# Filling the constant rows of layer 1's key tiles by ScalarE activations instead of by copies of whole tiles

## The chip, the core and the metric

The kernel runs on one core of a Trainium2 chip. Time is device time in microseconds (us) of that core, from three runs of the same program; one further execution was recorded by the hardware profiler, and all rows below come from it. The engines are TensorE (PE, with its weight loads as PEld), VectorE (DVE), ScalarE (ACT), GpSimd (POOL) and SyncE (SP). SP issues every transfer of this kernel, in order, on one queue; the transfers then run on 16 DMA engines.

## The reference, cut to what matters

Two transformer layers with adaptive layer norm, in 32-bit floats, on 2 sequences of 512 tokens and 512 channels. Each layer is an attention part and a feed-forward part, each behind a layer norm whose scale and shift come from a small conditioning vector, and each added to the residual through a gate.

```python
x = L0_attn_hidden_states                                   # [2, 512, 512]
h = _layernorm(x) * (1 + ca) + sa
x = x + ga * _L0_attn_ref(h, ...)      # 32 heads of 128, gated, decaying linear attention in chunks of 128
h = _layernorm(x) * (1 + cb) + sb
x = x + gb * _L0_ffn_ref(h, ...)       # sign of the weights
h = _layernorm(x) * (1 + ca) + sa      # from here on with layer 1's sa, ca, ga, sb, cb, gb
x = x + ga * _L1_attn_ref(h, ...)
h = _layernorm(x) * (1 + cb) + sb
x = x + gb * _L1_ffn_ref(h, ...)       # 4 streams, 50 rounds of Sinkhorn
```

The change is in layer 1's attention: 32 query heads of 16 channels, 8 key heads, each key head shared by 4 query heads, with a rotation by position and a softmax over all 512 keys.

```python
q = _rope(xq, cos, sin); k = jnp.repeat(_rope(xk, cos, sin), REP, axis=2)
scores = jnp.einsum('bqhd,bkhd->bhqk', q, k) / jnp.sqrt(jnp.float32(D))
probs = jax.nn.softmax(scores.astype(jnp.float32), axis=-1)
out = jnp.einsum('bhqk,bkhd->bqhd', probs, v)
```

## The kernel before

**Precision.** PE takes its operands in a shorter float (fp32r). Where that is too coarse, a value is split into a high part (an ACT copy into fp32r) and a low part (the rest, by POOL or DVE), and three products are summed: high by high, low by high, high by low. `halves` (L206) splits weights so, `exact` (L449) activations, `passes` (L226) makes the products.

**Layer 0's attention** is walked in 64 units, one for a group of four heads, a sequence and a chunk of 128 tokens (loop at L1374). A unit makes scores (`sps`), decays (`dec`, from `gb`, which SP broadcasts out of DRAM), mixes (`yps`), a gate (`gps`, `gate`, L471), a state (`cps`, `state`, L517), turns the result (`ztp`, `turn`, L562) and projects it out (`ops`, `project_out`, L577). `keys_of`, `query_of` and `values_of` project the next group's keys, queries and values (`pps`) meanwhile. Weights come from memory into the pool `raw` (four buffers, `raw_tile`, L198): `wk0`, `wq0`, `wv0` for the projections, `wg0` for the gate, `wo0` for the output. A buffer is free again when ACT has made the high part and POOL the low part.

**From layer 0 to layer 1.** With unit n goes `tail(n)` (L691): layer 0's feed-forward part and layer 1's norm, chunk by chunk. When the norm of a sequence is done, `project_kv` and `project_q` (L682, L686) project keys, values and queries of layer 1; `rope_halves` (L664) rotates them (shuffle and sums on DVE, one product on POOL), splits them into `hi1` (two buffers) and `lo1`, and writes both to DRAM, `k_dram` and `q_dram`, in an order of 48 rows a head (high, low, high for keys, high, high, low for queries), so that one matmul makes all three products. From unit 53 on (`FIRST`) pieces of layer 1's attention are worked beside the units.

**Layer 1's attention** goes through 16 entries of `order`: a sequence, half the queries, two of the 8 key heads. Each entry has two key tiles of 128 rows by 512 keys, one for each key head s (`ks`). `keys1` (L792) fills rows 48s to 48s+47 from `k_dram`; `queries1` (L799) fetches the query tiles `qs`. `maxima` (L833) makes scores `s` with rows 0 to 95 (L842) and their maxima `m` on DVE (L846); the negated maxima, split into high and low, go through PE (`mt`), ACT (`mm`) and a transfer (L862) into rows 96 to 99 of `qs`. `weigh` (L864) makes the scores again with 100 rows (L876), and ACT their exponentials `pt` (L881); `outputs` (L886) multiplies with the values into `op`. `weigh` runs up to 10 pieces behind `maxima` (`LAG`).

For this the key tiles need constant rows: zero where the other key head lies, zero or one in rows 96 to 99. Two rows of ones add the maximum's high and low part of that head. They are written once per tile, by `layer1_keys` (L740): for each s one load of a constant tile of 128x512 from DRAM (`c_keys1`) into `raw`, one ACT copy into a buffer of `hi1` (the local name is `empty`), and one transfer of the whole tile from there to each key tile. There are three sets of tiles, j = 0, 1, 2. Sets 0 and 1 are asked for at L711, within the loop over the two sequences in `tail`, so the call stands in the program twice; the second time gives new tiles, and those are used. Set 2 is asked for by the first `keys1` (L788). A tile is used again for later entries, with only its 48 rows replaced.

```python
KS, KM = 96, 100                 # rows of a key tile: keys; keys and constants
def key_tile(i):
    return i % 2 if i < TWO else (i - TWO + 2) % 3     # TWO is 0
...
if n == FIRST - 1:               # in tail(n), inside "for b in range(B)"
    layer1_keys()
```

**The feed-forward part of layer 1** (`streams0`, `streams1a`, `streams1b`, L1212 on) is a chain of small DVE and POOL instructions (the Sinkhorn rounds). The first half runs beside the attention; the last runs alone at the end and closes with PE and DVE products (`mix`).

**Order.** No queue's order is written out by hand. A planner places all instructions of all engines by its own estimates and by priorities (`tc.high_priority`); `anchor`, `behind` and `gated` add order without data, so that the work beside a unit keeps its place. `layer1_keys` at L711 stands within `behind`: its instructions may not be placed before the anchor of their engine. The call from `keys1` has no such bound. The rotation table of layer 0, `rope` (128x2x512, L353, loaded at L1339), stays in place to the end.

Of the kernel before, what the change touches and what calls it, by code (L numbers as in the profile page):

```python
# [9 lines left out]
FP = mybir.dt.float32  # L10
FR = mybir.dt.float32r
# [20 lines left out]
AF = mybir.ActivationFunctionType  # L32
# [4 lines left out]
P = 128  # L37
B, L, HID = 2, 512, 512
# [14 lines left out]
def tile_adaln(ctx: ExitStack, tc: tile.TileContext, a: dict, out: bass.AP):  # L53
    nc = tc.nc
# [24 lines left out]
    def keep(shape):  # L79

        m = int(np.prod(shape[1:]))
        t = room0[0:shape[0], used0[0]:used0[0] + m]
        used0[0] += m
        if len(shape) == 2:
            return t
        names = "abc"[:len(shape) - 1]
        return t.rearrange(
            f"p ({' '.join(names)}) -> p {' '.join(names)}", **{n: k for n, k in zip(names, shape[1:])}
        )
# [61 lines left out]
    def temp(shape, dt, name, bufs=2):  # L151
        return wk.tile(shape, dt, name=name, bufs=bufs)

    def bank(shape, name, bufs=2):
        return psp.tile(shape, FP, name=name, bufs=bufs)
# [42 lines left out]
    def raw_tile(load):  # L198
        raw = raws.tile([P, KC * P], FP, name="raw")
        nc.sync.dma_start(out=raw, in_=load)  # L200
        return raw
# [149 lines left out]
    gn = keep([P, 1])  # L351
    nc.sync.dma_start(out=gn, in_=a["gnorm"])
    rope = ck.tile([P, 2, L], FP, name="rope0")  # L353

    ps = bank([64, HID], "mps")
    for kc in range(KC):
# [334 lines left out]
    def tail(n):  # L691
# [4 lines left out]
        for b in range(B):  # L696
            c = n - ends[b]
            with behind():
                if -3 <= c < 1:
                    load_ffn(c + 3)  # L700
                    if c == -2:
                        load_ffn_rows(b)
                elif c == 5:
                    load_l1(b)
                elif 6 <= c < 8:
                    load_l1q(2 * c - 12)
                    load_l1q(2 * c - 11)
                    if c == 7:
                        load_rope1()
                if n == FIRST - 1:  # L710
                    layer1_keys()  # L711
# [24 lines left out]
    ksd = {}  # L736
# [2 lines left out]

    def layer1_keys(js=(0, 1)):  # L740
        for s in range(2):
            empty = temp([P, L], FR, "hi1")
            nc.scalar.copy(empty, raw_tile(a["c_keys1"][s]))
            for j in js:
                ksd[j, s] = temp([P, L], FR, f"ks{j}{s}")
                nc.sync.dma_start(out=ksd[j, s].bitcast(FP), in_=empty.bitcast(FP))

    steps = [(g, b) for g in range(KV0 - AHEAD) for b in range(B)]
    steps += [(g, b) for b in range(B) for g in range(KV0 - AHEAD, KV0)]
# [36 lines left out]
    def key_rows(i):  # L786
        j = key_tile(i)
        if j == 2 and (2, 0) not in ksd:  # L788
            layer1_keys((2,))
        return [ksd[j, s] for s in range(2)]  # L790
# [583 lines left out]
    for n, u in enumerate(units):  # L1374
        g, b, c = u["at"]
        s = n // NC
# [127 lines left out]
```

## Time and profile before

| What | us |
|---|---|
| Runs | 1404.83, 1406.62, 1407.78 (median 1406.62) |
| The profiled execution, and its span | 1401.8, 1400.0 |
| PE busy | 1245.7 (89%) |
| DVE busy | 1159.8 (83%) |
| ACT busy | 831.5 (59%) |
| POOL busy | 775.8 (55%) |

The page gives for each engine its busy time in the span. Its 40 slices are read as tenths:

```profile
PE   5979999999999999999988999799999889994128
DVE  7998668687677687787899977688799979898887
ACT  5457576476376466666665656557567467664128
PEclk9989999999999999999999999999999999997568
DMA  8022241231142343324333317523203231200001
```

A slice is 35 us. The first is the start, which loads; layer 0 fills slices 1 to some 30 with PE full; from slice 25 on layer 1's attention runs beside it, and alone from about slice 31; the last four slices are the Sinkhorn chain. PE reaches 9 in nearly all slices but the end. A group of instructions by source line, for instance, reads as line, engine, operation, what it writes and reads with sizes, how often, busy time, mean ns of one, and the idle time of the engine just before with what ended it; here the ACT copy, and the engine that is second busiest:

```profile
L743 ACT CAST hi<-raw 128x512 fp32r<-128x512 f32 x6 | 3.7, 616 | 5.5 <-DMA raw<-in_wv 5.0 <-DMA raw<-in_c_keys 0.4
L846 DVE TENSOR_REDUCE m<-s 128x1 f32<-128x512 f32 x256 | 166.4, 673 | 18.6 <-PE s L842 18.3
```

### The profile page before, as it was taken

To read this page: it belongs to the slowest core of one execution; us is meant where nothing else is said; L and a number is where in the kernel's file an instruction comes from. 1 tells how busy PE (TensorE), PEld (TensorE's weight loads), DVE (VectorE), ACT (ScalarE), POOL (GpSimd) and SP (SyncE) were. 2 spreads that over 40 slices of the span, in tenths; PEclk is the share of its full clock that TensorE was granted. 3 is DMA by queue.
4 is the path that set the end of the run, shared out by engine and by line. 5 is a ranking of instruction groups with operands and counts; after the bars stand their busy time and mean duration, and the time that the engine had idled before them with its cause. 6 is when DMAs were issued, how large, how long until landed. Compare 5 with 4: busy or idle time off the path is not lost. (4 is left out here: it accounts for less than half of the span.)

```text
span 1400.0 us, 22901 instructions
## 1 busy us (share of the span) xinstructions
PE 1245.7 (89%) x7168; PEld 992.1 (71%) x7168; DVE 1159.8 (83%) x2969; ACT 831.5 (59%) x2354; POOL 775.8 (55%) x1169
## 2 busy tenths in 40 slices
PE   5979999999999999999988999799999889994128
PEld 3758888788788778888866777577676666663117
DVE  7998668687677687787899977688799979898887
ACT  5457576476376466666665656557567467664128
POOL 4454374364264367577777748545242655558861
PEclk9989999999999999999999999999999999997568
DMA  8022241231142343324333317523203231200001
GB/s 256 23 65 60 88 121 30 68 107 53 53 118 57 92 120 106 98 68 124 118 114 91 98 53 241 170 67 91 90 24 113 71 111 52 59 11 1 1 16 46
DMA packets 95377, 117.13 MB, mean 84 GB/s; under 512 B 10828, under 2 KB 50508, under 8 KB 95256
## 3 DMA queue, kind: packets, MB, share of 16 engines
q1 hardware_dynamic: 95256, 115.67, 27.7%
q8 instruction: 57, 0.93, 0.3%
q14 instruction: 64, 0.52, 0.1%
HBM read 102.11 MB, written 10.64 MB: 81 GB/s over the span
## 5 line engine op out<-in xcount | busy, mean ns | idle before, releaser
L846 DVE TENSOR_REDUCE m<-s 128x1 f32<-128x512 f32 x256 | 166.4, 673 | 18.6 <-PE s L842 18.3
L67 ACT ACTIVATE pt<-s 128x512 f32<-128x512 f32 x256 | 136.9, 602 | 33.3 <-PE s L876 31.7
L447 POOL TENSOR_TENSOR q<-xcos,rot 128x512 f32<-128x512 f32 x64 | 92.8, 1450 | 61.6 <-DVE xcos L445 57.1
L67 ACT ACTIVATE sg<-sg 128x512 f32<-128x512 f32 x128 | 80.6, 632 | 68.5 <-DVE sg L478 66.8
L876 PE MATMUL s<-qs,ks 100*128 100x256 f32 x512 | 103.3, 306 | 11.0 <-DMA qs<-mm 7.4
L842 PE MATMUL s<-ks,qs 96*128 96x512 f32 x256 | 103.6, 437 | 9.7 <-DVE m L846 7.5
L515 POOL TENSOR_TENSOR gb<-gb,q 128x512 f32<-128x512 f32 x48 | 63.2, 1319 | 77.7 <-ACT gb L67 68.7
L232 PE MATMUL pps<-hh,wq_h 128*128 128x512 f32 x256 | 103.2, 403 | 1.7 <-ACT vT L766 1.1
L876 PEld LDWEIGHTS s<-qs,ks 100*128 100x128 f32 x512 | 80.9, 195 | 33.5 <-ACT pt L67 8.9
L232 PE MATMUL gps<-wg_h,hh 128*128 128x512 f32 x256 | 101.8, 400 | 2.9 <-ACT wg_h L209 2.7
L232 PE MATMUL ops<-wo_h,zh 128*128 128x512 f32 x256 | 101.5, 397 | 1.7 <-ACT zh L570 1.0
L232 PE MATMUL ops<-wo_h,zl 128*128 128x512 f32 x256 | 100.8, 394 | 0.7 <-DVE zl L571 0.7
L232 PE MATMUL pps<-hl,wq_h 128*128 128x512 f32 x256 | 101.3, 396 | 0.0
L232 PE MATMUL pps<-hh,wq_l 128*128 128x512 f32 x256 | 101.2, 395 | 0.0
L232 PE MATMUL gps<-wg_l,hh 128*128 128x512 f32 x256 | 101.2, 395 | 0.0
L232 PE MATMUL gps<-wg_h,hl 128*128 128x512 f32 x256 | 100.6, 393 | 0.0
L232 PE MATMUL ops<-wo_l,zh 128*128 128x512 f32 x256 | 99.9, 390 | 0.0
L67 ACT ACTIVATE dec<-dec,room 128x128 f32<-128x128 f32 x256 | 83.0, 398 | 21.8 <-POOL dec L495 21.7
L548 PE MATMUL yps<-v,dec 128*128 128x128 f32 x512 | 94.2, 280 | 1.8 <-DVE xcos L445 1.0
L495 POOL TENSOR_SCALAR_AFFINE_SELECT dec<-gb 128x512 f32<-128x512 f32 x64 | 49.1, 768 | 80.7 <-DMA gb<-g_dram 51.8
L522 POOL TENSOR_TENSOR xw<-v,room 128x512 f32<-128x512 f32 x48 | 55.2, 1163 | 68.5 <-ACT v L462 64.3
L558 DVE SCALAR_TENSOR_TENSOR z<-yps,ss,sg 128x128 f32<-128x128 f32 x256 | 71.9, 340 | 24.0 <-ACT ss L67 23.8
(323 smaller groups left out, 3968.5 us busy)
## 6 DMA issues: line engine op xcount, KB each, us to landing
gb<-g_dram SPq DMA_DIRECT2D x64, 256.0 KB
raw<-in_wq SPq DMA_DIRECT2D x56, 256.0 KB
raw<-in_wg SPq DMA_DIRECT2D x48, 256.0 KB
raw<-in_wo SPq DMA_DIRECT2D x48, 256.0 KB
raw<-in_wmod SPq DMA_DIRECT2D x40, 256.0 KB
qs<-q_dram SPq DMA_DIRECT2D x64, 96.0 KB
q_dram<-hi SPq DMA_DIRECT2D x16, 256.0 KB
raw<-in_wk SPq DMA_DIRECT2D x14, 256.0 KB
```

The source lines that it names most:

```text
L67: ins = nc.scalar.activation(o, i, func, **kw)
L232: nc.tensor.matmul(ps, lhsT=l, rhs=r, start=i == 0, stop=i == n - 1)
L447: nc.gpsimd.tensor_tensor(dst, sp(xc_), sp(rot), ALU.add)
L495: anchor["pool"] = nc.gpsimd.affine_select(out=dec, in_=gb, pattern=[[0, REP0], [1, P]], compare_op=ALU.is_ge, fill=-1e30, base=0, channel ...
L515: nc.gpsimd.tensor_tensor(gb, gb, q[:, c], ALU.mult)
L522: nc.gpsimd.tensor_tensor(xw, u["v"][:, c, :].unsqueeze(1).to_broadcast(sh4), wdc[:, c, r0:r0 + REP0].unsqueeze(2).to_broadcast(sh4), ALU. ...
L548: nc.tensor.matmul(yps[:, h, :], lhsT=u["pr"][:, h, :], rhs=u["v"][:, c, :], start=True, stop=not c)
L558: nc.vector.scalar_tensor_tensor(z[:, h, :], yps[:, h, :], ss[:, h:h + 1], sg[:, h * P:(h + 1) * P], ALU.mult, ALU.mult)
L842: anchor["pe"] = nc.tensor.matmul(ps, lhsT=st["qs"][rp][0:KS, i, qt * P:(qt + 1) * P], rhs=st["ks"][s][0:KS], start=True, stop=True,).ins
L846: anchor["dve"] = nc.vector.tensor_reduce(st["m"][:, 2 * qt + s, i:i + 1], ps, AX.X, ALU.max, negate=True).ins
L876: nc.tensor.matmul(ps[:, j, :], lhsT=st["ks"][s][0:KM, kt * P:(kt + 1) * P], rhs=st["qs"][rp][0:KM, i, :], start=True, stop=True,)
```

## The change

Two columns of 128 values (`empty`, one for each s) are loaded at the start from the first column of each constant tile. `layer1_keys` then writes each key tile with one ACT instruction: an identity activation of the first half of `rope`, times 0.0, plus the column as bias, so that each row of the tile holds its constant. The constant tiles' loads, the ACT copies into `hi1` and the transfers from there to the key tiles are gone. Where the function is called is unchanged.

```diff
     rope = ck.tile([P, 2, L], FP, name="rope0")
+    empty = keep([P, 2])
+    for s in range(2):
+        nc.sync.dma_start(out=empty[:, s:s + 1], in_=a["c_keys1"][s, :, 0:1])
...
     def layer1_keys(js=(0, 1)):
         for s in range(2):
-            empty = temp([P, L], FR, "hi1")
-            nc.scalar.copy(empty, raw_tile(a["c_keys1"][s]))
             for j in js:
                 ksd[j, s] = temp([P, L], FR, f"ks{j}{s}")
-                nc.sync.dma_start(out=ksd[j, s].bitcast(FP), in_=empty.bitcast(FP))
+                nc.scalar.activation(ksd[j, s], rope[:, 0, :], AF.Identity, bias=empty[:, s:s + 1], scale=0.0)
```

## The prediction

> **What bounds the kernel now.** I read the page's busy shares first: TensorE (PE) is busy 89% of the span, VectorE (DVE) 83%, ScalarE (ACT) 59%. So what delays PE for good costs time, unless it is PE's idle time anyway. Then the busy time by stage, because the change touches one place, the hand-over from layer 0 to layer 1 (the edited tiles are written from 840 us on). Columns: stretch, its length, then busy time of PE, weight loads, DVE, ACT, POOL, then granted clock, DMA share, GB/s.
>
> ```profile
> 800.00:830.00 30.00, 28.32 (x145) 23.69 (x144) 26.44 (x55) 19.04 (x58) 13.54 (x11) 1.00 0.24 70
> 830.00:850.00 20.00, 20.00 (x95) 16.51 (x95) 12.33 (x21) 11.65 (x22) 14.63 (x15) 1.00 0.45 146
> 850.00:870.00 20.00, 17.94 (x85) 14.69 (x83) 15.81 (x25) 13.54 (x35) 15.00 (x13) 0.91 0.72 232
> 870.00:890.00 20.00, 14.35 (x64) 11.14 (x62) 10.01 (x19) 4.91 (x17) 9.77 (x8) 0.90 0.77 235
> 890.00:910.00 20.00, 18.09 (x74) 13.36 (x72) 18.48 (x34) 15.00 (x42) 12.77 (x11) 0.93 0.44 121
> ```
>
> From 850 to 910 every compute engine sags, the transfers stand at 0.72 and 0.77, and the clock falls to 0.90. This is a stage that waits for transfers inside a kernel that does not. The waits from 835 to 910 say for which (waiter <- releaser: total, times, longest):
>
> ```profile
> ACT wg_h L209 <- DMA raw<-in_wg: 13.7, 3, 6.0
> DVE z L558 <- ACT ss L67: 6.0, 1, 6.0
> ACT hi L743 <- DMA raw<-in_wv: 5.0, 1, 5.0
> PE gps L232 <- ACT wg_h L209: 2.7, 1, 2.7
> PE ztp L566 <- DVE z L558: 2.7, 1, 2.7
> PE cps L232 <- DVE xwl L454: 2.1, 1, 2.1
> ```
>
> ACT stands behind the gate weights (wg), PE behind ACT. `hi L743` is the copy that the change removes; while it stands, ACT's queue stands. The order of SP's queue shows why wg is late:
>
> ```profile
> 844.48 3.59 SPq L746 DMA_DIRECT2D ks<-hi  x4
> ...
> 853.15 1.12 SPq L746 DMA_DIRECT2D ks<-hi  x2
> 854.36 1.34 SPq L678 DMA_DIRECT2D k_dram<-hi  x2
> ...
> 876.24 0.43 SPq L200 DMA_DIRECT2D raw<-in_wg  x1
> ...
> 882.62 0.53 SPq L746 DMA_DIRECT2D ks<-hi  x1
> ...
> 884.77 1.81 SPq L200 DMA_DIRECT2D raw<-in_wg  x1
> ```
>
> One queue, in order: key-tile copies stand ahead of the projected keys (854) and between the gate weights (876 to 885). PE after the first of its three stalls:
>
> ```profile
> 861.83 0.50 PE L232 MATMUL cps<-xwl,kth 128*128 128x512 f32 x1 [2.06 <-DVE xwl L454]
> 863.57 0.63 PE L232 MATMUL pps<-hl,wq_h 128*128 128x512 f32 x1
> 865.92 0.40 PE L232 MATMUL pps<-hl,wq_h 128*128 128x512 f32 x1
> ```
>
> After 2.06 us of idling a matmul takes 0.63 us, and 0.40 again some 4 us on.
>
> **What is removed.** layer1_keys runs three times (twice for tiles 0 and 1, once for tile 2): 6 loads of c_keys and 10 copies ks<-hi, 256 KB each, 4.2 MB. In 830 to 910 the rates above move 20 us x (146+232+235+121) = 14.7 MB, so 29% of the stage's bytes go; at 235 GB/s they are 17.8 us of transfers. On SP they took 6.8 us (ks<-hi) and 2.6 us (c_keys) between 836 and 888. On ACT six CASTs at 0.616 us go (3.7 us). Their tiles also shared two buffers, `hi1`, with the layer-1 projections, and the four `raw` buffers with the weights; both are relieved.
>
> **What is added.** Ten ACTIVATEs of 128x512, bias from a column, source in SBUF. The trace has none of that form: bounds are the CAST from SBUF (0.616) and L661's ACTIVATE with a bias column from PSUM (0.685); each occupies the queue 0.52 or 0.58 us until the next. I take 0.58, for the bias column: 5.8 us, 2.7 more than six CASTs at 0.52. And two loads of 128 four-byte elements, 0.33 to 0.49 us each on SP by the gnorm and gate loads.
>
> **What moves.** The planner places the whole kernel anew; the built order shows where.
> - Two ACTIVATEs (tile 2) go to the start, on ACT between the second and third chunk's ht. There ACT was free at 20.66 us. The gate load, issued at 15.27, was read at 21.77 without a wait; the columns, issued behind rope and two of the xin, about 14.6, should by that land by 21.1. So the third chunk is late by 1.2 to 1.6 us. Against that, hh of the fourth chunk now precedes an xn on DVE: in the trace ht was ready at 24.95 and its hh ran only at 27.17, so up to 1.8 us earlier. DVE is 98 to 100% busy from 20 to 60 us with the same work. Bounds -1.8 to +1.6; I take 0.
> - Eight go to about 803 to 810 us, 4.6 us where ACT has no gap (19.04 of 30 overall, full from 795 to 810). Behind them on ACT: rstd, sg, the state copy, ht, zh. Walking the new order with the trace's durations, zh moves from 807.0 to about 811, and zl on DVE ends near 812.9. PE, which used to take z at 809.6, now does the gate's and state's matmuls first and comes to z at 812.3. Bound: 0 to +1; I take 0. Placed later, they would have hit PE.
> - On SP, with the copies gone, k_dram is issued right after v_dram, and the four wg loads come before q_dram. Projected keys: hi at about 841 (its DVE sum ended at 840.8) instead of 853.0. Wg: they now wait for `raw` buffers that POOL's splits free, about 851 to 859, instead of 876 to 885.
> - On PE the gate's matmuls move ahead of pps<-wq,wk, and the first layer-1 score stands after 3747 matmuls instead of 3803.
>
> **The sum.** PE's idle time from 850 to 910 is 2.06 + 5.65 + 1.91 = 9.6 us. At the rate of 800 to 850 (1.68 in 50) 60 us would have 2.0 anyway: 7.6 to win. The slow clock: six 512-wide matmuls from 863.00 to 865.69 took 2.69 us against 6 x 0.227 = 1.36 at the usual pitch; likewise 5 from 884.16 (2.16 against 1.14) and 7 from 889.43 (3.56 against 1.59). Together 4.3. Ceiling 11.9 us. What is late next: POOL, whose splits, rope products and lo's queue up (I count 37 us of its work from 835 on, so the last q's lo near 872, against 875.5 to 876.8 now, but with the gate splits already done), and its q_dram writes must land before the first score. I leave one stall of the first kind, 2.06 + 1.33 = 3.4. Gain 8.5 us. Ends: 0 (all of it hidden) and 11.9.
>
> After 910 PE is at 94% to 1270, and the tail (1270 to 1400, a VectorE chain that starts when attention ends) keeps its order within a few places, so the gain carries through. Against the profiled execution, 1401.8 us (span 1400.0 and 1.8 around it): 1393.3. That execution lies 4.8 us under the median of the three runs, 1406.6; so in their terms **1398**.
>
> **A rule weighed.** Row: slow matmuls follow gaps of 2.06, 2.72 and 2.73 us. The Trainium skill (TensorE: Matmul & The Clock Gate, Part 1) lets the clock fall only after an idle window of about 3.4 us; by that these gaps would cost no clock and the sum would be 7.6 - 2.1 = 5.5, thus 1401. The measured rows decide. A rule against the change: ScalarE: Activation LUTs, Rules for kernel authors, sends adds and multiplies to VectorE. But from 800 to 830 DVE is busy 26.4 of 30 and ACT 19.0; by the rule, eight fills at hh's 0.43 would put 3.4 us onto the fuller engine, and the sum would fall to about 5.
>
> **The rivals.**
> 1. *The gap closes and is handed back* (20%). From 910 to 1270 DVE is busy 316.6 of 360 us and PE 337.2; maxima, weights and outputs wait on each other there, PE idles 22.8 us. If the earlier start only finds those waits longer, half or all goes: 1402 to 1407. For it: the same two engines stay full. Against: the order meets the old one again soon after (after 4106 matmuls), with the same work behind.
> 2. *Slower* (15%). From matmul 4660 to 5590 (about 1090 to 1240 us) the planner has shuffled scores and outputs. PE waits there 7.4 us in 8 goes for qs<-mm, the maxima's trip by DMA, out of 20 such issues; each lands in 1.9 us on the chain. If a shuffle leaves less between issue and use, each further exposure costs 1.9: five take the gain, six more than 0.2%, eight give 1406.6 - 8.5 + 15.2 = 1413. For it: these distances were only just long enough. Against: shuffles also lengthen them.
> 3. *More* (7%): the whole ceiling and the start's 1.8 us: 1393.
> 4. *It does not do what it says*: excluded, the built order has none of the 16 transfers, ten ACTIVATEs, two columns.
>
> **How the numbers follow.** My forecast, gain 5 to 12, has 58%: own range 1394 to 1402. What a measurement can tell from no change is 0.2%, 2.8 us. Rival 1 splits into 9% faster and 11% same. Faster 58 + 7 + 9 = 74%, same 11%, slower 15%. Range: down to rival 3 with a late shuffle in its favour (1390), up to all handed back with the start's 1.6 on top and a little of rival 2 (1409).
>
> **What would show it.** Right: L746 gone; ten L747 rows near 0.69 us; PE idle from 850 to 910 down from 9.6 to about 4, clock above 0.95; wg loads issued some 20 us earlier and ACT's 13.7 us wait for them nearly gone; the first `s` matmul near 872 to 878 instead of 897. Wrong: ht of the third chunk beyond 24 us; PE waiting for zl or cps near 812; the sag still there behind POOL; more than twelve waits of PE for qs<-mm.

## The result, and the profile after

The changed kernel takes 1412.97 us (median of six runs, 1411.92 to 1417.09) beside 1405.13 us for the kernel before on the same chip: a ratio of 1.0081, 95% interval 1.0056 to 1.0106. I had forecast 1398.0, 1390 to 1409, and faster. It is slower, outside the range. The profiled execution took 1411.92 us, with a span of 1409.9 us (before: 1401.8 and 1400.0), so the pair of traces shows 9.9 us of loss.

The same stretches of time that the prediction showed of before, in the changed kernel (columns: stretch, length, busy time of PE, weight loads, DVE, ACT, POOL, granted clock, DMA share, GB/s):

```profile
800.00:830.00 30.00, 30.00 (x156) 25.39 (x155) 24.46 (x53) 23.62 (x68) 13.20 (x11) 1.00 0.25 72
830.00:850.00 20.00, 20.00 (x96) 16.60 (x95) 10.67 (x22) 11.09 (x21) 15.82 (x16) 1.00 0.31 93
850.00:870.00 20.00, 18.66 (x97) 15.21 (x97) 15.63 (x28) 12.75 (x40) 16.84 (x13) 1.00 0.56 165
870.00:890.00 20.00, 12.98 (x48) 9.34 (x46) 14.84 (x24) 5.10 (x11) 10.77 (x8) 0.81 0.74 221
890.00:910.00 20.00, 15.09 (x59) 12.05 (x59) 14.98 (x27) 10.80 (x30) 10.04 (x9) 0.76 0.21 58
```

The transfers are fewer, and the sag has not gone: it has moved 20 us later and is deeper. PE idles 1.34 + 7.02 + 4.91 = 13.3 us from 850 to 910 (9.6 before), at a clock of 0.81 and 0.76. From 890 on the transfers stand at 0.21, so it is not bytes that PE waits for there. The waits from 835 to 910:

```profile
POOL dec L498 <- DMA qs<-q_dram: 10.1, 1, 10.1
...
PE sps L232 <- ACT qh L456: 9.3, 1, 9.3
ACT dec L67 <- POOL dec L498: 8.9, 2, 8.5
...
ACT wg_h L209 <- DMA raw<-in_wg: 4.6, 1, 4.6
```

ACT's wait for the gate weights has shrunk from 13.7 to 4.6 us, as forecast. A new chain stands in its place: PE waits 9.3 us for qh, ACT stands behind dec's exponentials, and those wait for POOL's `dec`, which waits 10.1 us for a transfer. The row names the transfer that landed last by the profile, but `dec` reads gb, the broadcast of the gate's running sum. SP's queue shows where the gb loads stood:

```profile
852.27 0.42 SPq L200 DMA_DIRECT2D raw<-in_wg  x1
...
861.17 0.56 SPq L200 DMA_DIRECT2D raw<-in_wg  x1
...
878.36 1.93 SPq L681 DMA_DIRECT2D q_dram<-hi  x2
880.39 1.33 SPq L200 DMA_DIRECT2D raw<-in_wo  x1
881.81 1.09 SPq L681 DMA_DIRECT2D q_dram<-lo  x1
882.96 1.34 SPq L496 DMA_DIRECT2D gb<-g_dram  x2
```

The wg loads moved some 20 us forward, from 876 to 885 down to 852 to 863. The first gb load for the same group of heads did not: 882.96 now, 883.92 in the kernel before, whose row is

```profile
883.92 0.80 SPq L493 DMA_DIRECT2D gb<-g_dram  x1
```

The gb loads now stand on SP's queue behind the rows of layer-1 queries on their way to q_dram. POOL got on with `dec` at 890.84, and PE, which had done its other work by then, took the scores' matmul at 894.91:

```profile
875.05 0.70 PE L843 MATMUL s<-ks,qs 96*128 96x512 f32 x2 [2.03 <-DMA qs<-q_dram]
...
894.91 0.80 PE L232 MATMUL sps<-qh,kh 128*128 128x512 f32 x1 [9.32 <-ACT qh L456]
```

To see where 9.9 us arise I follow rows that both traces have. Times in us; zh, the 51st, is ACT's L573 (before L570), rc is DVE's reciprocal of `finish`, L922 (L921), of which there are 32.

| | before | after | difference |
|---|---|---|---|
| PE's first ops | 111.4 | 114.3 | +2.9 |
| zh, the 45th | 684.7 | 689.1 | +4.4 |
| zh, the 51st | 790.7 | 790.8 | +0.1 |
| rc, the 5th | 1029.5 | 1032.8 | +3.3 |
| rc, the 7th | 1052.9 | 1056.2 | +3.3 |
| rc, the 15th | 1149.4 | 1155.7 | +6.3 |
| rc, the 32nd | 1273.7 | 1284.2 | +10.5 |

The start costs 3 to 4 us, and a stretch with idle time on PE before 790 takes it back. The hand-over (51st zh to 5th rc) takes 242.0 us instead of 238.8. The largest part, 7.2 us, is lost after 1053 us, 150 us behind the edit: 7th to last rc take 228.0 us instead of 220.8.

### The profile page after: what moved, and what is told of

Its sections match the earlier page's. It is cut to its first block, busy times and chain, and to the rows that moved or that the text cites. A ratio compares the mean times of both kernels' runs of the same rounds, so it can differ in the third digit from the quotient of the medians.

```text
span 1409.9 us, 22944 instructions
## 1 busy us (share of the span) xinstructions
PE 1256.2 (89%) x7168; PEld 997.5 (71%) x7168; DVE 1155.9 (82%) x2969; ACT 835.6 (59%) x2358; POOL 779.1 (55%) x1169
## 2 busy tenths in 40 slices
DMA packets 93362, 112.94 MB, mean 80 GB/s; under 512 B 10861, under 2 KB 50541, under 8 KB 93241
## 5 line engine op out<-in xcount | busy, mean ns | idle before, releaser
L551 PEld LDWEIGHTS yps<-v,dec 128*128 128x128 f32 x512 | 80.5, 196 | 13.9 <-issue 5.1
```

The lines of the kernel that those rows point to most:

```text
L551: nc.tensor.matmul(yps[:, h, :], lhsT=u["pr"][:, h, :], rhs=u["v"][:, c, :], start=True, stop=not c)
```

## The experiments

Three theories. *Theory 1*: at the hand-over one wait took the place of another, the gb loads behind the query writes. *Theory 2*: the planner's shuffle of the late stretch costs, and it would cost without the edit too. The third is the start. Below, "hand-over" is the 51st zh to the 5th rc and "late" the 7th to the last rc, each from the run's one profiled execution; times are medians.

| kernel | hand-over | late | time, us | ratio to before, 95% |
|---|---|---|---|---|
| before | 238.8 | 220.8 | 1401.9 to 1405.1 | |
| after | 242.0 | 228.0 | 1412.97 | 1.0081, 1.0056 to 1.0106 |
| e1 after, query writes of two groups off SP | 240.1 | 219.2 | 1402.65 | 1.0001, 0.9977 to 1.0025 |
| e2 before, columns only | 235.2 | 224.7 | 1407.02 | 1.0029, 1.0001 to 1.0057 |
| e3 before, called once | 240.3 | 220.9 | 1408.65 | 1.0035, 1.0007 to 1.0062 |
| e4 after, called once | 242.2 | 233.8 | 1417.41 | 1.0086, 1.0052 to 1.0119 |
| e5 before, late order shuffled | 243.8 | 228.9 | 1421.69 | 1.0125, 1.0094 to 1.0156 |
| e6 before, late order kept | 237.5 | 217.9 | 1405.71 | 1.0004, 0.9983 to 1.0025 |
| e7 after, late order of before | 243.3 | 221.0 | 1406.14 | 1.0015, 0.9989 to 1.0041 |
| e8 after, late order shuffled | 241.9 | 231.6 | 1414.52 | 1.0074, 1.0045 to 1.0103 |
| e9 before, copies doubled | 249.3 | 221.1 | 1412.43 | 1.0064, 1.0042 to 1.0086 |
| e10 after, all query writes off SP | 230.6 | 218.8 | 1397.50 | 0.9943, 0.9921 to 0.9966 |
| e11 before, once and writes off SP | 238.2 | 225.4 | 1403.64 | 0.9982, 0.9952 to 1.0013 |
| e12 after, five raw buffers | 239.9 | 223.6 | 1408.53 | 1.0043, 1.0015 to 1.0072 |
| e13 before, writes off SP | 245.2 | 222.4 | 1407.64 | 1.0034, 1.0014 to 1.0055 |
| e14 before, three groups off SP | 244.4 | 223.7 | 1405.68 | 1.0025, 1.0002 to 1.0048 |

One and the same program varies: 26 runs of before beside e1 to e4 lay between 1394.79 and 1411.26. A single profile therefore says where time went, and the medians say how much.

**e1, the gb loads set free.** In `rope_halves` of the changed kernel (`dst` is q_dram for `wq1`):

```diff
-                nc.sync.dma_start(out=dst[:, r:r + D1, :], in_=src.bitcast(FP))
+                (nc.sync if not (b == 0 and n == "wq1" and i >= 2) else nc.scalar if src is hi
+                 else nc.gpsimd).dma_start(out=dst[:, r:r + D1, :], in_=src.bitcast(FP))
```

> The changed kernel, but the layer-1 query rows of head groups 2 and 3 of the first batch row are written to q_dram from ScalarE's queue (hi) and GpSimd's queue (lo) instead of SyncE's, so that the two loads of the gate gb stand 15 places earlier on SyncE's queue. Theory 1 (at the hand-over one wait took the place of another: POOL's dec waits for gb, which stands on SP's queue behind these writes, and qh, sps and all of PE behind dec): PE's wait of 9.3 us at 885 to 895 shrinks to under 3 us, PE's idle time from 850 to 910 falls from 13.3 to under 8 us, and if that carries through, the time falls by 4 to 9 us, to 1404 to 1409. Theory 2 (the late stretch decides: the planner's shuffle of scores and outputs after 1040 us costs the 7 us, whatever happens at the hand-over): the gap closes all the same, but the time goes anywhere from 1403 to 1418, because the late order is shuffled anew. My prediction's theory (POOL itself is what is late): the wait for dec remains, 1413.

Measured: 1402.65, the whole loss gone. The gb loads go out at 869.73, and the 9.3 us wait of PE is no longer among the waits. But the trace does not put the gain where theory 1 had it:

```profile
870.00:890.00 20.00, 15.91 (x57) 12.04 (x58) 15.66 (x25) 8.89 (x26) 15.96 (x14) 0.83 0.80 249
890.00:910.00 20.00, 18.01 (x72) 12.80 (x71) 19.85 (x38) 10.88 (x36) 10.92 (x9) 0.83 0.31 92
```

PE's idle time from 850 to 910 falls to 6.4 us, and then it idles 6.4 us more from 910 to 980 (4.2 in the changed kernel); the hand-over takes 240.1 us. Counted from the 51st zh, e1 reaches the 56th 5.2 us sooner than the kernel before (97.6 us against 102.8) and the 5th rc 1.3 us later: what was won is handed back, as rival 1 has it. At the 7th rc e1 is 3.4 us later than before, and the changed kernel 3.3. Only behind that do they part: 219.2 us to the end against 228.0. Here a comparison of the built orders tells why: from matmul 4106 to the end PE's order in e1 is that of the kernel before, place by place, while in the changed kernel some 740 places from 4660 on hold another matmul, 680 of them up to 5590. (The expectation of e5 says 964; a count by place cannot give that, as 4660 to 5590 has 931 places.) A small edit at the hand-over had thrown the planner back onto the old late order. That is for theory 2, but e1 changes two things at once.

**e2, the start alone.** The kernel before with the two column loads, read by nobody:

```diff
+    emptyc = keep([P, 2])
+    for s in range(2):
+        nc.sync.dma_start(out=emptyc[:, s:s + 1], in_=a["c_keys1"][s, :, 0:1])
```

> The kernel before, with the two column loads of the change added at the start and nothing reading them: the start is planned anew, all 16 transfers of the key tiles stay. Theory 1: nothing at the hand-over changes in kind, 1403 to 1407. A third theory (the change's loss is the start: the trace of after is 3.6 us late at 185 us): 1408 to 1409, if it is the loads and not the two ACTIVATEs behind them; by theory 1 that lateness is gone before 780 us, as in the trace of after. Theory 2 (a shuffle anywhere costs or wins up to 8 us by chance): anywhere from 1397 to 1413.

Measured: 1407.02. The reshuffled start is 5 to 6 us late from 250 to 640 us, more than in the changed kernel, and 1.5 us at the 51st zh. So lateness at the start is taken back before the hand-over here too, and it is not what the change lost. What this trace loses, it loses late (224.7): 4.9 us behind 1234 us, where the clock stands at half for 13.7 us against 3.4 in the kernel before, with PE's order that of before. The last section shows the same of e11.

**e3 and e4, made once.** The call for tiles 0 and 1 stands in `for b`; here it is made for one b only, in the kernel before (e3) and in the changed one (e4):

```diff
-                if n == FIRST - 1:
+                if n == FIRST - 1 and b == 0:
```

> The kernel before, with the call that makes key tiles 0 and 1 made once instead of twice: 2 loads, 4 copies ks<-hi and 2 CASTs fewer (1.5 MB of the 4.2 MB), no ACTIVATE and nothing at the start. My prediction's theory (the transfers bound the hand-over): a third of its gain, 1402 to 1403. Theory 1 (the next wait stands right behind): 1404 to 1408. Theory 2: anywhere from 1397 to 1413, with the difference arising after 1040 us.

> The changed kernel with that call made once: four of the ten ACTIVATEs fewer, the two columns and the two fills at the start stay. Theory 1: POOL's dec still waits for gb, 1411 to 1415. If the ACTIVATEs at 803 to 810 us were the cost (2.3 us of ACT go): 1410 to 1411. Theory 2: anywhere from 1403 to 1418, and the time of the hand-over (to 1040 us) as in the changed kernel within 2 us.

Measured: e3 1408.65 and e4 1417.41. Neither removal helps. In e4, 0.7 us of ACTIVATE each for four instructions is gone and its hand-over takes 242.2 us beside 242.0 in the changed kernel, so nothing shows that the fills at 803 to 810 us cost; it loses 13 us late, in an order that differs from the changed kernel's in some 260 places. In e3 1.5 MB of transfers are gone, the hand-over takes 240.3 instead of 238.8, and its late order, which differs from before's in some 200 places, costs nothing in its trace (220.9): not every shuffle costs.

**e5 to e8, the late order by itself.** The edit of e1 with other conditions gives four kernels: before and after, each with the late order kept or shuffled. The conditions (written `hi`, `lo` for the rows that leave SP's queue, the others staying on it):

```diff
 e5 (before): b == 0 and n == "wq1" and i >= 3, hi rows to nc.scalar
 e6 (before): b == 0 and n == "wq1" and i >= 3, lo rows to nc.gpsimd
 e7 (after):  b == 0 and n == "wq1",            lo rows to nc.gpsimd
 e8 (after):  b == 0 and n == "wq1" and i >= 3, lo rows to nc.gpsimd
```

> The kernel before with all its transfers; only the hi rows of the layer-1 query group 3 of the first batch row go to q_dram from ScalarE's queue instead of SyncE's. On PE this moves 234 places at the hand-over (matmuls 3645 to 4106), and it happens to give a late order like the changed kernel's from matmul 4660 on (of the changed kernel's 964 places of difference to before, most are shared). Theory 2, now that e1, which has the late order of before, lost nothing after 1056 us: the late order alone costs 6 to 10 us, so 1409 to 1414, with the lateness arising between 1100 and 1245 us, although nothing of the change is in this kernel. Theory 1 (the change's fills and the hand-over cost): 1402 to 1406.

> The same edit on the lo rows, to GpSimd's queue: 323 places at the hand-over differ from before, and from matmul 4106 on PE's order is that of before. Both theories: 1400 to 1406. If e5 and this one are both slow, the edit at the hand-over costs and not the late order.

> The changed kernel, the lo rows of all four query groups of the first batch row written from GpSimd's queue: another hand-over than e1's, and from matmul 4106 on PE's order is that of before. Theory 2: as e1, 1400 to 1406, and nothing lost after 1056 us. Theory 1: it depends on the hand-over alone; POOL's wait for gb before dec is about as long as in the changed kernel, so 1410 to 1414.

> The changed kernel, the lo rows of group 3 alone written from GpSimd's queue: at the hand-over 6 places on PE differ from the changed kernel, and from matmul 4660 on it has the late order of e4 (the called-once one), not that of before. Theory 2: 1412 to 1419, 8 to 14 us of it lost between 1056 and 1275 us. Theory 1: within 2 us of the changed kernel's 1413, and whatever differs arises before 1040 us.

Measured: kept, 1405.71 (before) and 1406.14 (after); shuffled, 1421.69 (before) and 1414.52 (after). The late order costs, whether the change is in the kernel or not: the kernel before, with all its transfers and none of the edit, is 1.25% slower in e5, and the changed kernel is the same as before within what is measured once its late order is kept. Not all of e5's loss is late: its trace is 15.6 us longer than that of before, 8.1 of it late and 5.0 at the hand-over (243.8 us). The cleaner pair is e7 and e8, with hand-overs of 243.3 and 241.9 us: 8.4 us lie between their medians, 10.6 between their late stretches. Over all sixteen kernels the late stretch takes 217.9 to 225.4 us where PE's late order is before's (or e3's) and 228.0 to 233.8 us in the four shuffled ones. e7 was told apart from theory 1 as well: POOL still waits 10.5 us for gb there, and the time is not 1410.

What the shuffled order does is seen at 1110 to 1150 us, where the second batch row's layer-1 projection runs beside attention. PE's larger waits there, first in the kernel before, then in the changed kernel:

```profile
1121.51 0.69 PE L842 MATMUL s<-ks,qs 96*128 96x512 f32 x1 [3.30 <-DVE m L846]
...
1134.74 0.48 PE L876 MATMUL s<-qs,ks 100*128 100x256 f32 x2 [2.07 <-DMA qs<-mm]
```

```profile
1123.09 0.50 PE L877 MATMUL s<-qs,ks 100*128 100x256 f32 x2 [2.81 <-ACT os L909]
...
1139.01 0.77 PE L877 MATMUL s<-qs,ks 100*128 100x256 f32 x2 [2.62 <-DMA qs<-mm]
```

and e5:

```profile
1130.41 0.80 PE L842 MATMUL s<-ks,qs 96*128 96x512 f32 x1 [3.47 <-DVE m L846]
1145.20 0.48 PE L876 MATMUL s<-qs,ks 100*128 100x256 f32 x2 [4.12 <-DMA qs<-mm]
```

The first wait of e5, for m, the kernel before has too (3.30 us), so the shuffle did not bring it. The second wait is for the maxima's short transfer, mm, which goes out straight behind the last query writes of the second batch row. Changed kernel, SP's queue:

```profile
1131.27 1.21 SPq L681 DMA_DIRECT2D q_dram<-hi  x2
1132.58 0.59 SPq L681 DMA_DIRECT2D q_dram<-lo  x1
1134.05 0.67 SPq L863 DMA_DIRECT2D qs<-mm  x1
```

From its issue to PE's next matmul 4.96 us pass (6.12 in e5, from 1139.08), with the transfers at 0.63 from 1130 to 1139. In the kernel before it went out at 1130.99, ahead of two of those writes, and 3.75 us later PE went on, having waited 2.07 us. From 1050 on, PE waits for qs<-mm 7.1 to 7.5 us in eight goes in kernels whose order is kept (before, e1, e6), and 7.0, 12.0, 10.6 and 9.8 us in ten to twelve goes in the changed kernel, e4, e5 and e8. Stretches at half clock follow such gaps. With the clock records of the traces, PE's idle time and its busy time times one minus the clock come to 27.3 us late in before and 24.4 to 32.2 in the other kernels with the order kept (or e3's), and to 30.9, 37.2, 33.8 and 36.0 in the changed kernel, e4, e5 and e8. The two ranges meet. What is left of the late stretch, PE's busy time reckoned at full clock, keeps them apart: 192.1 to 193.9 us in the twelve kernels, 195.1 to 197.2 in the four. Why the same matmuls take longer in the shuffled order is not shown.

**e9, what bytes cost.** The kernel before with each copy made twice, the second from ScalarE's queue:

```diff
                 nc.sync.dma_start(out=ksd[j, s].bitcast(FP), in_=empty.bitcast(FP))
+                nc.scalar.dma_start(out=ksd[j, s].bitcast(FP), in_=empty.bitcast(FP))
```

> The kernel before with each of the ten key-tile copies made a second time, from ScalarE's queue: 2.6 MB more transfers in the stage that my prediction says waits for transfers, and from matmul 4246 on PE's order is that of before. My prediction's theory (the stage waits for transfers; 4.2 MB less is worth 8.5 us): 2.6 MB more cost about 5 us, 1407 to 1412, lost between 840 and 960 us. Theory 2 with the hand-over bound by its chain of waits, not by bytes: 1402 to 1406.

Measured: 1412.43, 0.64% slower, all of it at the hand-over (249.3 us, +10.5; late 221.1 as before). The waits from 835 to 910 and the stretch say by what:

```profile
ACT wg_h L209 <- DMA raw<-in_wg: 13.8, 2, 13.0
...
PE gps L232 <- ACT wg_h L209: 10.7, 1, 10.7
```

```profile
890.00:910.00 20.00, 14.06 (x51) 10.96 (x52) 10.14 (x18) 10.07 (x24) 12.40 (x11) 0.70 0.92 256
```

So the chain that I named in the prediction, transfers to wg to ACT to PE, grows when the kernel before is given more transfers: 2.6 MB on top cost 7.8 us by the medians, nearly what I had given for 4.2 MB less. That bytes alone do it is not shown. ScalarE issues ten more transfers here, and the gate weights that ACT waited for were issued at 888.74 (876.24 to 884.77 in the kernel before), behind query writes on SP's queue.

**e10, the loss undone.** The changed kernel with the condition `b == 0 and n == "wq1"`, hi rows to ScalarE's queue and lo rows to GpSimd's:

> The changed kernel, the hi rows of all four layer-1 query groups of the first batch row written from ScalarE's queue and the lo rows from GpSimd's: the loads of gb stand 23 places earlier on SyncE's queue than in the changed kernel, and from matmul 4106 on PE's order is that of before. Theory 1 in its weaker form (the late order cost the 7 us, the wait for gb the rest, and with it gone the transfers' removal pays): the stretch from 790 to 1030 us shrinks from 242 to 234 or less, 1396 to 1400. If the next wait in line (queries through q_dram, splits on GpSimd) takes its place again: 239 to 242 there, 1401 to 1406.

Measured: 1397.50, ratio 0.9943 (0.9921 to 0.9966): faster than both. The gb loads go out at 855.57 and 861.67 instead of 882.96, the late order is before's (218.8 us), and the hand-over takes 230.6 us, 8.2 less than before.

```profile
850.00:870.00 20.00, 19.66 (x102) 16.25 (x102) 18.05 (x26) 13.47 (x42) 19.98 (x16) 1.00 0.69 202
870.00:890.00 20.00, 14.00 (x48) 10.53 (x47) 19.25 (x30) 10.27 (x22) 12.00 (x12) 0.82 0.58 189
890.00:910.00 20.00, 17.91 (x82) 13.95 (x82) 17.71 (x40) 10.79 (x39) 12.99 (x10) 0.92 0.33 96
```

POOL's wait for gb is down to 2.6 us, and no wait of PE in 835 to 910 is longer than 2.3 us. The profiled execution is the fastest of ten (1391.80); by the medians the gain is 7.1 us. Of the 8.2 us at the hand-over, 4.0 are idle time of PE and 3.6 busy time lost to half clock. But the wait for gb is not what sets e10 apart from e1, where that wait of PE is gone too and the hand-over takes 240.1 us: POOL's `dec` ran at the same time in both (e1, then e10), though gb was issued 14 us sooner in e10.

```profile
884.29 1.23 POOL L498 TENSOR_SCALAR_AFFINE_SELECT dec<-gb 128x512 f32<-128x512 f32 x2
```

```profile
884.62 1.23 POOL L498 TENSOR_SCALAR_AFFINE_SELECT dec<-gb 128x512 f32<-128x512 f32 x2
```

What else it is in moving the writes of groups 0 and 1 that pays, no run here shows.

**e11 to e14, whose gain is that?** e11 is e3 with the edit of e1. e12 is the changed kernel with `RAW = 5`. e13 and e14 make e10's move in the kernel before: e13 for all query and key rows of the first batch row, e14 for query groups 0 to 2.

```diff
 e13 (before): b == 0,                          hi rows to nc.scalar, lo rows to nc.gpsimd
 e14 (before): b == 0 and n == "wq1" and i < 3, hi rows to nc.scalar, lo rows to nc.gpsimd
```

> The kernel before, tiles 0 and 1 made once, and the query rows of groups 2 and 3 written from ScalarE's and GpSimd's queues: 1.5 MB of transfers fewer and no fills on ScalarE, and from matmul 4240 on PE's order is that of before. Theory 2: nothing lost late, 1400 to 1406, in contrast to e3 (1408.7, made once, with another late order). If fewer transfers without fills pay: 1397 to 1400.

> The changed kernel with five buffers for raw weights instead of four, so that weight loads on SyncE's queue wait less for GpSimd's splits, and what stands behind them too; the order up to 800 us differs in 600 places on PE, and from matmul 4240 on it is that of before. Theory 2: nothing lost after 1056 us, 1400 to 1406. If waits for buffers are what holds the hand-over: 790 to 1030 us in 236 or less, 1396 to 1400.

> The kernel before with all its key-tile transfers; the rows of keys and queries of the first batch row are written to DRAM from ScalarE's (hi) and GpSimd's (lo) queues, as in e10 and the keys too; from matmul 4106 on PE's order is that of before. If e10's gain is that of the move of the writes alone: 790 to 1030 us in 229 to 233, 1395 to 1400 as e10. If it takes both, the move and the change's fewer transfers: 235 to 241 there, 1401 to 1406.

> The kernel before, the query rows of groups 0, 1 and 2 written from ScalarE's and GpSimd's queues, those of group 3 from SyncE's; from matmul 4567 on PE's order is that of before. The same two readings: by the move alone 230 to 235 in 790 to 1030 us and 1396 to 1401, by both together 236 to 241 and 1402 to 1406.

Measured: e11 1403.64, e12 1408.53, e13 1407.64, e14 1405.68; hand-overs of 238.2, 239.9, 245.2 and 244.4 us. The move of the writes without the change gains nothing (in e13 ACT waits 18.7 us for wg from 840 to 985, and POOL 14.4 us for gb). Fewer transfers without the fills, with two groups moved, gain nothing that is clear of noise (e11, ratio 0.9982, 0.9952 to 1.0013). e12's fifth buffer does not help either: its gb loads go out at 894.92, later than in the changed kernel, and more than 800 places before 800 us differ, so it is a weak test. So the gain stands only where both are, the change and all the query writes of the first batch row off SP's queue. e13 moves the key rows too and e14 leaves one group of queries where it was, so neither is e10's move to the letter, and that it takes both is likely, not shown.

## Why the prediction was wrong, step by step

- *What bounds the kernel* held in part. The stage waits for transfers: doubling the copies lengthened the hand-over by 10.5 us (e9), through the chain that I had read from the waits. How much of that is bytes and how much the place on SP's queue, e9 does not tell apart.
- *Removed and added* held. 117.13 MB became 112.94, L746 is gone. The ten fills take 718 ns each (705 to 754), above both rows that I bounded them with (616 and 685); taking four away did not shorten the hand-over (e4).
- *What moves.* Right: hi for k_dram at 841, the wg loads at 852 to 863 (forecast 851 to 859), the first layer-1 score at 875.05 (forecast 872 to 878; 897.1 before), PE 30.00 of 30 busy over the eight fills. The start lies outside its bounds, -1.8 to +1.6: it runs 3 to 4 us late from 171 to 676 us. The third chunk's ht, which I had late, is not why: it started at 20.64 us, and at 21.54 in the kernel before. The lateness cost nothing, because a stretch before 790 us had the slack, which I had not named.
- *The sum: "I leave one stall of the first kind, 2.06 + 1.33 = 3.4"*. This step failed first. I had found what the change moves forward, and looked for what is late next among POOL's splits and the query writes. I did not follow gb, an input of the group of heads whose gate weights now came 20 us sooner. It stood on the same queue behind those query writes, at 882.96, unmoved. The stall was 9.3 us and the hand-over gained nothing (242.0 against 238.8, where kernels with before's transfers lie between 235.2 and 245.2). That this wait alone held the gain back is not shown: with it gone and little else moved (e1) the hand-over still takes 240.1 us. In e10 it gains 8.2 us, close to the 8.5 of the sum, but not in the way of the sum: PE still idles 8.4 us from 850 to 910, where I expected about 4.
- *"After 910 ... so the gain carries through"*. This step failed by more. It rested on PE being full and the tail's order being kept; the late shuffle in between cost 7.2 us in the trace, and 8.1 in e5, which has none of the change. With the late order kept (e1, e7) the changed kernel is as fast as before within what is measured. So this step is the loss, and the step before it the missing gain.
- *Rival 2* named that shuffle, the place (1090 to 1240 us) and a time (1413; measured 1412.97), and I gave it 15%. Its mechanism was half of it: the waits for qs<-mm grew in e4, e5 and e8, by 2.4 to 4.6 us, but not in the changed kernel (7.0 us in ten goes; 7.4 in eight before), where the largest new wait was 2.8 us for ACT's os, and half clock grew most. That the time agrees is luck: its sum holds the gain of 8.5 us, which did not come, and eight more waits of 1.9 us for qs<-mm, which did not come either.
- *The rule weighed.* The rows again decide: half clock follows gaps of 2.03 to 2.81 us in the changed kernel, below the idle window of about 3.4 us that the Trainium skill asks for (TensorE: Matmul & The Clock Gate, Part 1). Its figure returns as the length of a stretch at half clock and as the step of the grid on which the clock changes, as the last section shows. The rule for VectorE was not tried.

Open: which of the shuffled places cost. In the changed kernel's late 7.2 us half clock takes 4.9 more than before (13.3 against 8.4) and PE's idle time 1.3 less (17.6 against 18.9); the remaining 3.6 us are busy time reckoned at full clock, which no row here explains. Open too is what held the hand-over in e1. And one profile per kernel can't settle differences of two or three us at the hand-over.

## What to carry to other kernels

When a change brings work forward, list every input of that work and its place on the in-order queue that issues it; the one input that was not moved is the next wait. (Taking that one wait away, as e1 does, need not pay: the next stands behind it.) Where a planner places everything anew, an edit also changes the order far behind it, and that can outweigh the edit: before a time is put down to the edit, hold it against a kernel with the same far order. Here a few neutral edits gave such kernels, and one of them, with the writes issued from the queues of the engines that make the rows, turned a loss of 0.8% into a gain of 0.6%.

## What the runs showed of the hardware

Read in windows of 1 us, the clock falls to 0.50 for 3.4 us or a multiple of it, and it does so about when PE goes on after a gap: 0.4 us before to 1.8 us after in the changed kernel's two large gaps above. In the kernel before, the gap that ended at 1121.51 was followed by half clock from 1121.7 to 1125.1; in the changed kernel, the one that ended at 1139.01 by half clock from 1138.6 to 1145.4, two such lengths. PE at 1128 to 1146 us in before and at 1130 to 1150 in the changed kernel:

```profile
1128.00:1135.00 7.00, 4.93 (x35) 4.01 (x32) 5.91 (x18) 4.03 (x9) 4.09 (x12) 1.00 0.55 154
1135.00:1139.00 4.00, 4.00 (x36) 1.64 (x35) 0.80 (x2) 0.60 (x1) 0.66 (x3) 0.57 0.45 148
1139.00:1146.00 7.00, 7.00 (x64) 4.96 (x64) 6.21 (x18) 5.66 (x12) 2.91 (x12) 1.00 0.11 30
```

```profile
1130.00:1139.00 9.00, 6.39 (x56) 3.94 (x55) 5.98 (x18) 3.34 (x8) 3.98 (x16) 0.88 0.63 220
1139.00:1146.00 7.00, 6.99 (x46) 4.27 (x47) 1.54 (x4) 2.16 (x4) 0.66 (x3) 0.54 0.02 6
1146.00:1150.00 4.00, 4.00 (x24) 3.12 (x22) 4.00 (x12) 3.63 (x8) 1.33 (x6) 1.00 0.19 51
```

And the same gaps don't always do it. At the end of attention PE's order in e11 is that of before. Before, two gaps and what follows; e11, the same two gaps and what follows:

```profile
1242.00:1244.00 2.00, 1.26 (x9) 0.91 (x8) 2.00 (x11) 0.06 (x1) 1.13 (x5) 1.00 0.01 4
1250.00:1252.00 2.00, 1.35 (x7) 0.85 (x7) 2.00 (x9) 0.42 (x2) 1.30 (x6) 1.00 0.01 4
1254.00:1258.00 4.00, 4.00 (x47) 2.58 (x47) 4.00 (x15) 2.72 (x8) 2.67 (x13) 1.00 0.00 0
```

```profile
1248.00:1250.00 2.00, 1.29 (x8) 0.89 (x7) 2.00 (x8) 0.09 (x1) 0.77 (x4) 1.00 0.02 8
1256.00:1258.00 2.00, 1.34 (x7) 0.72 (x6) 2.00 (x9) 0.72 (x2) 0.88 (x5) 1.00 0.01 4
1260.00:1264.00 4.00, 4.00 (x34) 2.34 (x37) 3.77 (x16) 1.86 (x4) 2.60 (x12) 0.57 0.00 0
```

With 0.74 and 0.65 us of idling in two windows of 2 us the clock held at 1.00 in before; with 0.71 and 0.66 it fell to 0.57 over 4 us in e11. So the idle time alone does not settle it. The clock records of the traces say more. In all sixteen, every change of the clock lies on a grid of 3.41 us that runs through the whole trace. Take the windows of that grid from 120 to 1262 us that are at full clock, in all sixteen traces: the next one was at half clock after 72 of 72 windows with 2.0 us or more of idle time on PE, after 100 of 426 with 0.5 to 2.0 us, and after 2 of 4615 with less. So it matters how much of a gap falls into one window: of the 2.81 us that ended at 1123.09 in the changed kernel, 1.25 lie in one and 1.56 in the next. For the windows between 0.5 and 2.0 us no rule comes out of these traces.

A window at half clock costs at most 1.7 us, by estimate: half of 3.4, where PE is busy all through. It goes with the 1.2% by which runs of one program differ: of the 26 runs of before beside e1 to e4, the five fastest (1397.8 us on average) had a mean granted clock of 0.949, the five slowest (1408.9) of 0.943. That the clock is the cause there, and not the gaps that it follows, is not shown.
